# A graph network's edge pass: one gathered tile in 24 built from columns in SBUF, and gathers of 125 rows throughout

## The chip, the cores and the metric

The kernel runs on one core of a Trainium2 chip. The metric is the device time of one execution in microseconds; lower is better. A core has five engines with instruction streams of their own: PE (TensorE, matmul), DVE (VectorE), ACT (ScalarE), POOL (GpSimd) and SP (SyncE). Here SP issues the plain transfers and POOL the indirect ones; 16 DMA engines carry both.

## The reference

12,500 nodes with 64 features, 412,500 edges with 32 features, sorted by receiver. With h the normalised and rectified node features:

```python
def _L0_gnn_ref(node_features, edge_features, senders, receivers, W1, b1, W2, b2, Wa1, ba1, Wa2, ba2, Wu1, bu1, Wu2, bu2):
    act = jax.nn.swish
    msg_in = jnp.concatenate([node_features[senders], node_features[receivers], edge_features], axis=-1)
    messages = act(msg_in @ W1 + b1) @ W2 + b2
    att_logits = act(msg_in @ Wa1 + ba1) @ Wa2 + ba2
    att = jax.nn.softmax(att_logits, axis=0)
    messages = messages * att
    aggregated = jax.ops.segment_sum(messages, receivers, num_segments=node_features.shape[0])
    upd_in = jnp.concatenate([node_features, aggregated], axis=-1)
    return act(upd_in @ Wu1 + bu1) @ Wu2 + bu2
h = jnp.maximum(_layernorm(x, axis=-1), 0.0)
x = x + _L0_gnn_ref(h, edge_attr_32, src, dst, ...)
```

The softmax runs over all edges, so the kernel keeps a running maximum. All data are float32.

## The kernel before

**Tables.** A node phase computes h and keeps its transpose in SBUF (`hT`, the even and the odd nodes on either half of the partitions). It writes two tables of 128 columns to DRAM: `ts_d`, what a node gives as a sender, and `tr_d`, what it gives as a receiver. The 128 columns are 64 of the attention's first layer and 64 of the message's.

**Groups.** The edges are cut into tiles of 125 (`EP`); 8 tiles (`K`) make a group, and there are 413 groups (`NG`). `one_pass` runs over them.

**`load(g)`** (L524) is called two groups ahead. It takes one of 7 `gather` buffers, and POOL issues 8 indirect transfers into it (L533), one for each tile j: row e of tile j is the row of `ts_d` that edge e's sender names. Even j fetch 125 rows, odd j 126 (`WIDE`); the row in excess falls on a partition that nothing reads. POOL runs ahead of all other engines until there is no free buffer; a buffer is free when `end` of its group has read it. In every fourth group SP loads edge features into `eo` (L544) and receivers into `dbs` (L547). For each group SP loads two windows of `tr_d` into `wins` (L554), one of three buffers, at an address that a register holds. DVE compares the receivers with the window's rows (L558), which gives a one-hot matrix in `eo`; on PE four products (L562, each in two instructions) of `eo` with `wins` give, in the PSUM tile `pe`, the receivers' and the edges' part for all 8 tiles.

**`begin(g)`** (L570): DVE adds `pe` to the gathered rows (L573), ACT takes the tanh into `pe` (L576). **`end(g)`** (L578): DVE makes the messages (L586) and the attention logits (L592, L594, L597); in every fourth group `top` and `weigh` move the running maximum, with two exponentials on ACT (L627, L630).

**`sum_up`** (L714) sums an earlier group by node: `by_node` builds weights on DVE (L640) and multiplies them on PE into `sp` (L646); `out_of` copies `sp` with ACT (L652); `project` multiplies by W2 and Wu1 on PE (L657); `put` adds on DVE to `sums` (L671, L675) and notes the maximum in `stand` (L678), both at register addresses.

**Order.** Most instructions are kept in the order in which they are written (`pin`); each engine works through its own in that order. In an iteration of the loop (L738) ACT has the tanh, the copy of `out_of`, the first `burst`, the second `burst`, and `weigh`'s exponentials where a batch ends.

**Columns.** `chosen` names groups whose last tile (j = 7) is not gathered. `numbers(g)`, `places(g)`, `columns`, `burst` and the branches on `g in chosen` in `load` and `begin` serve them. In this kernel `chosen` is empty (L472), and none of this issues an instruction.

Of the kernel before, what the change touches and what calls it, by code (L numbers as in the profile page):

```python
# [44 lines left out]
F32 = mybir.dt.float32  # L45
# [8 lines left out]
P = 128  # L54
EP = 125
# [3 lines left out]
C = 2 * U  # L59
S1 = U + 1  # L60
K = 8
# [12 lines left out]
EVERY = 3  # L74
PHASE = 1
SLOTS = (((0, 24), (24, 24)), ((48, 24), (72, 12)), ((84, 24), (108, 17)))
ROUND = 12582912.0
WIDE = 126
EPS = 1e-5
NEG = -3.0e38  # L80
BIG = 3.0e38
# [9 lines left out]
def gnn_kernel(ctx: ExitStack, tc: tile.TileContext, n_edges, x, src, src_row, dst, dst_row, first, edge,  # L91
# [73 lines left out]
    with tc.tile_pool(name="node1", bufs=1) as node1, \  # L165
# [134 lines left out]
        for c, nn in chunks:  # L300
            tr = node.tile([P, CB, C], F32, name="tr")[:, :nn, :]
            for b in range(0, nn, 4):
                n = min(4, nn - b)
                pn = node_ps.tile([P, 4, C], F32, name="pn", bufs=4)
                for i in range(0, n, 2):
# [7 lines left out]
        pin(nc.scalar.dma_start(hT_d, hT))  # L313

    one_pass(tc, n_edges, locals())
    again = nc.values_load(wrong[0:1, 0:1], min_val=0, max_val=1,
                           skip_runtime_bounds_check_because="it is the outcome of a comparison")
# [76 lines left out]
def one_pass(tc, n_edges, v):  # L394
    nc = tc.nc
    NB, T, NG, NP, NT = (v[k] for k in ("NB", "T", "NG", "NP", "NT"))
    ident, iota_w, bj, dloc, src_full, base_sb, real, unreal, far, wrong = (
        v[k] for k in ("ident", "iota_w", "bj", "dloc", "src_full", "base_sb", "real", "unreal",
                       "far", "wrong"))
    ts_d, tr_d, bq_d, xb_d, edge, dst_row = (  # L400
        v[k] for k in ("ts_d", "tr_d", "bq_d", "xb_d", "edge", "dst_row"))
    wa2, ba2_c, w2b, wu1a, wu2h, we, gather = (
        v[k] for k in ("wa2", "ba2_c", "w2b", "wu1a", "wu2h", "we", "gather"))
# [8 lines left out]
    with ExitStack() as ctx:  # L412
# [38 lines left out]
        for w in wins:  # L451
            nc.vector.memset(w, 0.0)
            for r in range(2):
                rows = slice(WR + r * DE, WR + (r + 1) * DE)
                nc.vector.tensor_copy(w[rows, :, r, :], we[rows, None, :].to_broadcast([DE, 2, C]))
        with tc.tile_pool(name="work2", bufs=2) as work2, \
# [3 lines left out]
            pes, gss, lgs, ps_, psums, sps, pps, ees, mts, nums, cols = ({} for _ in range(11))  # L460
# [8 lines left out]
            for h in range(2):  # L469
                nc.vector.tensor_copy(w2u[:, h, :], w2u_ps)  # L470

            chosen = set()  # L472

            def numbers(g):
                if g in chosen:
# [30 lines left out]
            def burst(g, k):  # L506
                for i in range(EVERY):
# [6 lines left out]
                           ap=[[C, NP + WR - SHIFT], [SHIFT * C, 2], [1, C]])  # L514

            def registers(g, engine, at, base=base_sb, top=NP - 1):
                n = min(NQ, NG + (base is not base_sb) - g)
                _, regs = nc.values_load_multi_w_load_instructions(
                    base[0:1, g:g + n], engines=[engine], min_val=0, max_val=top,
                    skip_runtime_bounds_check_because=WHY)  # L520
                for i in range(n):
                    at[g + i] = regs[i]

            def load(g):  # L524

                t = g * K
                if g % NQ == 0:
                    registers(g, ENG.SP, at_sp)
                full = gather.tile([P, K, C], F32, name="gs")
                gs = gss[g] = full[:EP]  # L530
                for j in range(K - (g in chosen)):
                    rows = WIDE if j % 2 == 1 else EP
                    nc.gpsimd.indirect_dma_start(  # L533
                        out=full[:rows, j, :], out_offset=None, in_=ts_d[:, :],
                        in_offset=bass.IndirectOffsetOnAxis(ap=src_full[:rows, t + j:t + j + 1], axis=0))
                if g % NQ == 0:
                    n = min(NQ, NG - g) * E2
                    eo = eos[g // NQ % 2]
                    i = g // NQ % 2
                    db = dbs[i * WR:(i + 1) * WR].bitcast(I32)  # L540
                    for i in range(g, min(g + NQ, NG)):
                        e = slice((i - g) * E2, (i - g + 1) * E2)
                        ees[i] = eo[:, e], db[:, e]
                    nc.sync.dma_start(eo[WR:, :n],  # L544
                                      edge[:, g * E2:g * E2 + n])
                    for r in range(2):
                        nc.sync.dma_start(  # L547
                            db[r * R:(r + 1) * R, :n],
                            bass.AP(tensor=dst_row.tensor, offset=dst_row[r:r + 1, g * E2:].offset,
                                    ap=[[0, R], [1, n]]))  # L550
                eo, db = ees.pop(g)
                win = wins[g % WINS]
                for r in range(2):
                    nc.sync.dma_start(win[r * R:(r + 1) * R, :, r, :],  # L554
                                      tr_w[bass.ds(at_sp[g], R), :, :])
                for h in range(2):
                    e = slice(h * E2 // 2, (h + 1) * E2 // 2)
                    pin(nc.vector.tensor_scalar(eo[:WR, e], db[:, e], bj[g // NQ % 2 * WR:(g // NQ % 2 + 1) * WR, g, h:h + 1], None,  # L558
                                                op0=ALU.is_equal))
                pe = pes[g] = pre_ps.tile([P, K, C], F32, name="pe")[:EP]  # L560
                for q in range(H):
                    pin(nc.tensor.matmul(pe[:, 2 * q:2 * q + 2, :], eo[:, q * EP:(q + 1) * EP],  # L562
                                         win[:, q // 2, :, :], start=True,
                                         stop=q < H - 1 or g not in chosen))
                if g in chosen:
                    to, _ = cols[g]
                    pin(nc.vector.scalar_tensor_tensor(to, nums[g], half, to, op0=ALU.is_equal, op1=ALU.mult))
                    pin(nc.tensor.matmul(pe[:, K - 1, :], to, stack, start=False, stop=True))
# [166 lines left out]
            for g in range(AHEAD):  # L735
                load(g)
            done = 0
            for g in range(NG):  # L738
# [18 lines left out]
                if g + AHEAD < NG:  # L757
                    load(g + AHEAD)
# [382 lines left out]
```

## Time and profile before

| | us |
|---|---|
| median of 3 runs | 5168.84 |
| the 3 runs | 5172.98, 5157.05, 5168.84 |
| the profiled execution | 5172.98 |
| its span, first to last instruction | 5171.3 |

| engine | busy us | share of the span | instructions |
|---|---|---|---|
| POOL | 3674.5 | 71% | 3329 |
| DVE | 3165.5 | 61% | 8745 |
| PE (matmul) | 2470.4 | 48% | 11247 |
| PEld (weight loads, beside matmul) | 1946.3 | 38% | 11247 |
| ACT | 608.2 | 12% | 1250 |

The mean granted TensorE clock is 0.595; the DMA engines are some 30% busy. "Busy" leaves out register, semaphore and DMA-issuing instructions of the sequencers, but counts POOL's indirect transfers, for which POOL itself works. In the page's lines of groups, the two numbers after the bar are the busy time in us and the mean of one instruction in ns; after the second bar stands the idle time of the engine just before them, and what ended it. In a timeline the columns are start and length in us, engine, line, operation, tiles, count, and in brackets the idle time before it.

### The profile page before, as it was taken

The numbers are of one execution on the slowest core, as the hardware profiler recorded it, in microseconds if no ns is written. First come the engines' busy times: TensorE is split into PE (matmuls) and PEld (weight loads), VectorE is DVE, ScalarE is ACT, GpSimd is POOL, SyncE is SP. The second block draws the span as 40 slices with busy tenths as digits, with TensorE's granted clock in tenths as the row PEclk, the third lists the DMA queues.
The fourth block names the chain that finished last, engine by engine and source line by source line (L and its number), as shares of the span: only waits on it lengthen the run. The fifth ranks groups of instructions, "written<-read, shape, count | busy, mean of one in ns | idle before, by whom it ended". The sixth has DMA issues, their size and how long they took to land. (4 is left out here: it accounts for less than half of the span.)

```text
span 5171.3 us, 46541 instructions
## 1 busy us (share of the span) xinstructions
PE 2470.4 (48%) x11247; PEld 1946.3 (38%) x11247; DVE 3165.5 (61%) x8745; ACT 608.2 (12%) x1250; POOL 3674.5 (71%) x3329
## 2 busy tenths in 40 slices
PE   5254544544454544444544544444444444444545
PEld 4243433433343433333333433333333333333435
DVE  6366666666665656565655656665656555655757
ACT  3011111111110111111110111111111111110112
POOL 4777677677677677777777777777777777777772
PEclk8555565665555556665655556665656555655656
DMA  7233333333333323323323322322323323323322
GB/s 242 64 80 74 78 88 74 79 80 78 75 74 70 71 64 73 73 67 72 73 66 70 73 67 69 74 67 70 72 65 73 73 64 73 73 65 72 73 66 69
DMA packets 315703, 393.24 MB, mean 76 GB/s; under 512 B 153249, under 2 KB 244478, under 8 KB 315042
## 3 DMA queue, kind: packets, MB, share of 16 engines
q0 software_dynamic: 211456, 214.45, 17.8%
q1 hardware_dynamic: 102594, 166.10, 13.1%
q10 hardware_dynamic: 1376, 9.67, 0.5%
q8 instruction: 92, 1.51, 0.1%
q14 instruction: 185, 1.52, 0.1%
HBM read 362.26 MB, written 25.72 MB: 75 GB/s over the span
## 5 line engine op out<-in xcount | busy, mean ns | idle before, releaser
L533 POOL DMA_INDIRECT gs<-ts_d,src_sb x3304 | 3657.3, 1107 | 1410.1 <-issue 1377.3
L562 PE MATMUL pe<-wins,eo 128*125 128x256 f32 x3304 | 1497.2, 631 | 1055.7 <-issue 453.6
L562 PEld LDWEIGHTS pe<-wins,eo 128*125 128x125 f32 x3304 | 1000.4, 317 | 1348.9 <-issue 518.5
L657 PE MATMUL mt<-ss,w2u 65*128 65x40 f32 x826 | 224.4, 369 | 1336.6 <-issue 703.3
L657 PEld LDWEIGHTS mt<-ss,w2u 65*128 65x128 f32 x826 | 209.4, 293 | 1536.3 <-issue 970.7
L640 DVE TENSOR_SCALAR wt<-iota_w,dloc,p 125x40 f32<-125x40 f32 x3304 | 760.1, 342 | 5.0
L646 PE MATMUL sp<-wt,acts 125*65 125x40 f32 x6608 | 714.6, 286 | 3.6 <-DVE wt L640 2.7
L646 PEld LDWEIGHTS sp<-wt,acts 125*65 125x65 f32 x6608 | 678.9, 205 | 7.7 <-DVE wt L640 3.4
L675 DVE TENSOR_TENSOR sums<-sums,mt 64x40 f32 x606 | 116.0, 191 | 854.1 <-remote 734.0
L576 ACT ACTIVATE pe<-gs 125x1024 f32<-125x1024 f32 x413 | 424.7, 1028 | 1600.3 <-DVE gs L573 759.1
L573 DVE TENSOR_TENSOR gs<-pe,gs 125x1024 f32<-125x1024 f32 x413 | 503.1, 1218 | 50.3 <-issue 30.7
L671 DVE SCALAR_TENSOR_TENSOR sums<-sums,scale,mt 64x40 f32 x220 | 56.1, 255 | 594.5 <-remote 446.3
L652 ACT COPY ss<-sp 65x40 f32<-65x40 f32 x413 | 77.4, 187 | 2543.9 <-remote 2380.3
L592 DVE SCALAR_TENSOR_TENSOR pe<-pe,gs 125x512 f32<-125x512 f32 x413 | 288.9, 699 | 14.0
L594 DVE TENSOR_TENSOR pe<-pe,w_all 125x512 f32<-125x512 f32 x413 | 288.7, 699 | 13.8
L586 DVE SCALAR_TENSOR_TENSOR acts<-pe,gs 125x512 f32<-125x512 f32 x413 | 285.6, 692 | 15.7 <-issue 3.1
L597 DVE TENSOR_REDUCE lg<-pe 125x8 f32<-125x512 f32 x413 | 284.0, 688 | 11.0
L558 DVE TENSOR_SCALAR eo<-dbs,bj 64x250 f32<-64x250 int32 x826 | 274.4, 372 | 16.1 <-DMA dbs<-in_dst_row_dram 7.8
L678 DVE COPY stand<-nmax 64x40 f32 x826 | 181.8, 220 | 2.0 <-issue 1.4
L616 PE MATMUL mt<-ident,mx 125*128 125x125 f32 x110 | 46.4, 421 | 269.7 <-remote 124.5
L623 DVE TENSOR_REDUCE gm<-mt 128x1 f32<-128x125 f32 x110 | 31.1, 282 | 200.7 <-remote 200.1
L357 DVE TENSOR_SCALAR bu<-mt,w_all 64x256 f32<-64x256 f32 (+1 forms) x50 | 23.9, 478 | 170.0 <-remote 124.6
(113 smaller groups left out, 571.3 us busy)
## 6 DMA issues: line engine op xcount, KB each, us to landing
gs<-ts_d,src_sb POOLq DMA_INDIRECT x3304
eo<-in_edge_dram SPq DMA_DIRECT2D x103, 500.0 KB
dbs<-in_dst_row_dram SPq DMA_DIRECT2D x206, 250.0 KB
wins<-tr_d SPq DMA_DIRECT2D x826, 32.0 KB
ts_d<-ts SPq DMA_DIRECT2D x5, 896.0 KB
tr_d<-tr ACTq DMA_DIRECT2D x5, 896.0 KB
hT_d<-hT ACTq DMA_DIRECT2D x1, 3136.0 KB
xt<-in_x_dram SPq DMA_DIRECT2D x24, 128.0 KB
```

The costliest lines, as they stand in the source:

```text
L533: nc.gpsimd.indirect_dma_start(out=full[:rows, j, :], out_offset=None, in_=ts_d[:, :], in_offset=bass.IndirectOffsetOnAxis(ap=src_full[:ro ...
L558: pin(nc.vector.tensor_scalar(eo[:WR, e], db[:, e], bj[g // NQ % 2 * WR:(g // NQ % 2 + 1) * WR, g, h:h + 1], None, op0=ALU.is_equal))
L562: pin(nc.tensor.matmul(pe[:, 2 * q:2 * q + 2, :], eo[:, q * EP:(q + 1) * EP], win[:, q // 2, :, :], start=True, stop=q < H - 1 or g not in ...
L573: pin(nc.vector.tensor_tensor(gss[g][:, :n, :], pes[g][:, :n, :], gss[g][:, :n, :], ALU.add))
L576: pin(nc.scalar.activation(pes[g], gss[g], AF.Tanh))
L586: pin(nc.vector.scalar_tensor_tensor(acts[g % ACTS][:, :, 0:U], th[:, :, U:C], 1.0, gs[:, :, U:C], op0=ALU.add, op1=ALU.mult))
L592: pin(nc.vector.scalar_tensor_tensor(att, th[:, :, 0:U], 1.0, gs[:, :, 0:U], op0=ALU.add, op1=ALU.mult))
L594: pin(nc.vector.tensor_tensor(att, att, wa2[:EP, None, :].to_broadcast([EP, K, U]), ALU.mult))
L597: pin(nc.vector.tensor_reduce(lgs[s][:, k:k + K], att, AX.X, ALU.add))
L640: pin(nc.vector.tensor_scalar(wt[:, j, :], iota_w[:EP, j // H, :], dloc[:, g * K + j:g * K + j + 1], p[:, k + j:k + j + 1], op0=ALU.is_equ ...
L646: pin(nc.tensor.matmul(sp, acts[g % ACTS][:, j, :], wt[:, j, :], start=j == 0, stop=j == K - 1))
L657: pin(nc.tensor.matmul(pp, w2u.rearrange("s h u -> s (h u)"), sps.pop(g), start=True, stop=True))
```

## The change

Three things differ. `chosen` holds every third group from 10 to 400 (131 groups). All gathers have 125 rows, and a chosen group has 7 of them. With `chosen` filled, the code that stood idle issues instructions:

- `numbers(g)`, seven groups ahead: SP loads the tile's 125 sender numbers into all 128 partitions.
- `places(g)`, six groups ahead: six small DVE operations turn them into places in `hT` and keep each number's lowest bit.
- `columns`, in the `burst`s of the three iterations from five to three groups ahead: a register load for each burst, then for each of the 125 edges a copy by ACT of one column (128 partitions x 1) of `hT` into `cols`, at a register's address.
- in `load(g)`: DVE keeps the half of the column that is the sender's and zeroes the other (L567), and PE multiplies the 125 columns with the stacked sender weights, onto the same PSUM tile.
- in `begin(g)`: L573 adds 7 tiles, and the eighth is copied from PSUM.

```diff
-            chosen = set()
+            chosen = {g for g in range(8, NG - 12) if g % EVERY == PHASE}
```

```diff
-                full = gather.tile([P, K, C], F32, name="gs")
-                gs = gss[g] = full[:EP]
+                gs = gss[g] = gather.tile([P, K, C], F32, name="gs")[:EP]
                 for j in range(K - (g in chosen)):
-                    rows = WIDE if j % 2 == 1 else EP
                     nc.gpsimd.indirect_dma_start(
-                        out=full[:rows, j, :], out_offset=None, in_=ts_d[:, :],
-                        in_offset=bass.IndirectOffsetOnAxis(ap=src_full[:rows, t + j:t + j + 1], axis=0))
+                        out=gs[:, j, :], out_offset=None, in_=ts_d[:, :],
+                        in_offset=bass.IndirectOffsetOnAxis(ap=src_sb[:, t + j:t + j + 1], axis=0))
```

What both kernels hold, and only the second one runs (`EVERY` = 3, `PHASE` = 1; `SLOTS` deals out the 125 columns as 24 and 24, 24 and 12, 24 and 17):

```python
            def columns(g, first, n):
                if g not in chosen:
                    return
                to, at = cols[g]
                _, regs = nc.values_load_multi_w_load_instructions(
                    at[0:1, first:first + n], engines=[ENG.Activation], ...)
                for i in range(n):
                    pin(nc.scalar.copy(to[:, first + i:first + i + 1], hT[:, bass.ds(regs[i], 1)]))

            def burst(g, k):
                for i in range(EVERY):
                    columns(g + 3 + i, *SLOTS[EVERY - 1 - i][k])
...
                if g in chosen:
                    to, _ = cols[g]
                    pin(nc.vector.scalar_tensor_tensor(to, nums[g], half, to, op0=ALU.is_equal, op1=ALU.mult))
                    pin(nc.tensor.matmul(pe[:, K - 1, :], to, stack, start=False, stop=True))
...
                n = K - (g in chosen)
                pin(nc.vector.tensor_tensor(gss[g][:, :n, :], pes[g][:, :n, :], gss[g][:, :n, :], ALU.add))
                if n < K:
                    pin(nc.vector.tensor_copy(gss[g][:, n, :], pes[g][:, n, :]))
```

More of the change, by code (lines that the diff above doesn't have):

```diff
@@ L77 @@
 ROUND = 12582912.0
-WIDE = 126
 EPS = 1e-5
@@ L396, in one_pass @@
     NB, T, NG, NP, NT = (v[k] for k in ("NB", "T", "NG", "NP", "NT"))
-    ident, iota_w, bj, dloc, src_full, base_sb, real, unreal, far, wrong = (
-        v[k] for k in ("ident", "iota_w", "bj", "dloc", "src_full", "base_sb", "real", "unreal",
+    ident, iota_w, bj, dloc, src_sb, base_sb, real, unreal, far, wrong = (
+        v[k] for k in ("ident", "iota_w", "bj", "dloc", "src_sb", "base_sb", "real", "unreal",
                        "far", "wrong"))
```

## The prediction

> **What bounds the kernel now.** I read the page first: totals, then the costliest groups.
>
> ```profile
> span 5171.3 us, 46541 instructions
> ...
> DVE  6366666666665656565655656665656555655757
> ACT  3011111111110111111110111111111111110112
> POOL 4777677677677677777777777777777777777772
> ...
> L533 POOL DMA_INDIRECT gs<-ts_d,src_sb x3304 | 3657.3, 1107 | 1410.1 <-issue 1377.3
> ```
>
> No engine is full. POOL is closest to being occupied: 3304 gathers, 3657.3 us busy, and 1410.1 us idle which is put down to "issue", that is, to nothing the profile shows. ACT does about a tenth of what it could. So I read POOL's timeline, at the first gathers and at a later pause:
>
> ```profile
> 51.22 1.38 POOL L533 DMA_INDIRECT gs<-ts_d,src_sb  x1 [48.81 <-issue]
> 52.90 1.00 POOL L533 DMA_INDIRECT gs<-ts_d,src_sb  x1 [0.30 <-issue]
> 54.20 1.21 POOL L533 DMA_INDIRECT gs<-ts_d,src_sb  x1 [0.30 <-issue]
> 55.71 1.00 POOL L533 DMA_INDIRECT gs<-ts_d,src_sb  x1 [0.30 <-issue]
> ```
>
> ```profile
> 2543.36 1.21 POOL L533 DMA_INDIRECT gs<-ts_d,src_sb  x1 [0.30 <-issue]
> 2544.88 0.99 POOL L533 DMA_INDIRECT gs<-ts_d,src_sb  x1 [0.31 <-issue]
> 2552.61 1.21 POOL L533 DMA_INDIRECT gs<-ts_d,src_sb  x1 [6.73 <-issue]
> ```
>
> The first gather is j = 0 with 125 rows, and lengths alternate: 125 rows take 1.21 us, 126 rows 1.00 us, and 0.305 us always lies between two. So a 125-row gather costs 1.519 us of POOL (twice the mean of 1107 ns, less 1.00, plus 0.305) and a 126-row one 1.305. Of the idle time, 48.8 us stand before the first gather and 3303 x 0.305 = 1007 us are this spacing. The rest, 1410 - 49 - 1007 = 354 us, are pauses like the one of 6.73 us. They come at a group's first gather, the one that takes a buffer: POOL has filled all seven and waits for `end` of the group seven back.
>
> What keeps the buffers? On DVE, L573 opens every group's second half:
>
> ```profile
> 2507.77 1.22 DVE L573 TENSOR_TENSOR gs<-pe,gs 125x1024 f32<-125x1024 f32 x1 [0.21 <-issue]
> 2518.57 1.22 DVE L573 TENSOR_TENSOR gs<-pe,gs 125x1024 f32<-125x1024 f32 x1
> 2546.31 1.21 DVE L573 TENSOR_TENSOR gs<-pe,gs 125x1024 f32<-125x1024 f32 x1
> 2553.84 1.23 DVE L573 TENSOR_TENSOR gs<-pe,gs 125x1024 f32<-125x1024 f32 x1 [0.19 <-issue]
> 2561.68 1.23 DVE L573 TENSOR_TENSOR gs<-pe,gs 125x1024 f32<-125x1024 f32 x1 [0.21 <-issue]
> 2568.89 1.21 DVE L573 TENSOR_TENSOR gs<-pe,gs 125x1024 f32<-125x1024 f32 x1
> ```
>
> Steps of 10.8 and 27.7 us, then 7.5, 7.8, 7.2. The short steps are DVE's own work (3165 us over 413 groups is 7.7). The long steps are waits for TensorE:
>
> ```profile
> 2529.64 0.19 DVE L675 TENSOR_TENSOR sums<-sums,mt 64x40 f32 x1 [9.85 <-remote]
> 2621.73 0.19 ACT L652 COPY ss<-sp 65x40 f32<-65x40 f32 x1 [14.00 <-remote]
> 2644.58 0.19 ACT L652 COPY ss<-sp 65x40 f32<-65x40 f32 x1 [21.48 <-remote]
> ```
>
> Both read PSUM that PE has to finish. So two things share the pace. POOL needs 4 x (1.519 + 1.305) = 11.3 us a group. The chain behind runs at 7.2 to 7.9 in quick spells, catching POOL up, and in laggard spells falls back until POOL has no buffer. A pause ends where a quick spell begins (2546 to 2553), and so it repeats. The span is POOL's issue time plus the pauses:
>
> 51.2 (start of the first gather) + 3304 x 1.412 = 4665 + 354 + 102.5 (from the last gather's start at 5068.8 to the end) - 1.4 (the last one, counted twice) = 5171. That execution took 5172.98, 1.7 more than its span and 4.1 over the median of 5168.84.
>
> **The change part by part.**
> (a) Rows: all gathers have 125 rows, so each costs 1.519.
> (b) Fewer gathers: groups 10, 13, ... 400 are chosen, 131 of them, each one gather short: 3173. POOL then needs 3173 x 1.519 = 4820, which is 155 more than 4665: 1652 odd gathers get 0.214 longer (+354), and 131 go (-199). A group costs 11.67 instead of 11.3 on average. This lies on POOL's line with nothing beside it.
> (c) ACT gets 125 copies of one column (L503) in each chosen group, each with an instruction that sets the address, and 6 register loads. No such copy is in the trace. From below: L627 to L630 on ACT start 0.11 apart in the timeline (2507.59 and 2507.70). Nearer: four DVE operations with register addresses, L675 and L678, start at 2512.57, 2512.68, 2512.87 and 2512.99, 0.14 apart. From above: 187 ns of L652 with nothing overlapped and an address instruction of 0.07 before it, 0.26. I take 0.14, the row that has register addresses too. A load: 0.34 (L518 on DVE). So 125 x 0.14 + 6 x 0.34 = 19.5 us a chosen group (15.8 to 34.5), 6.5 for each group on average; ACT goes from 608 to 608 + 131 x 19.5 = 3160 us. In an iteration ACT has 1.03 (tanh) + 0.19 + 6.5 = 7.7, at most 8.7 where 48 copies fall. Behind the copies on ACT wait weigh's exponentials and the next tanh, for which DVE's `end` waits. With short steps of 7.5 this makes them 8 to 9, still under POOL's 11.67, and in long steps ACT idles 14 to 21 us already. Cost on the path: nothing, covered by POOL's pace; without that cover, some 1 us in each of about 5 short steps of 8, 260 us.
> (d) DVE gets in a chosen group 5 operations on 1x125 (0.2 from start to start, as L624 to L626), one on 128x125 and L567 on 128x125 (0.28 each, L623), and L573 split into 896 columns and a copy of 128 (0.22 for the copy, L678, less 0.13 by the slope between 692 ns at 512 and 1218 at 1024). 1.7 us, 131 times 223 us, from 3165 to 3388 us in all. It fills short steps: the same cover, and 223 us without it. L567 waits for the last columns of ACT; behind it on DVE are the weights L640 and then PE's sp matmuls. The columns stand ahead of the tanh that DVE needs anyway, so it is not late first.
> (e) PE gets one product more per chosen group, two instructions of 0.42 (L856, 128x128 f32): 110 us, under PE's idle half, but laggard spells are PE's: up to 110 us if none of it hides; from below nothing.
> (f) SP gets 131 loads of 62.5 KB (L478), 0.32 us of issue each as `wins` L554. They stand behind the windows and ahead of the next group's; the numbers are wanted one iteration later. Nothing, or 131 x 0.32 = 42 us.
>
> [...] The last gather is issued at 5068.8 and the last L573 starts at 5118.3, so landing has tens of us to spare.
>
> **The sum.** Span 51.2 + 4820 + 354 + 102.5 - 1.5 = 5326; as a run 5328, and 4 less against the median: **5325**, 3.0% slower. The pauses are kept as they are: I see no reason in the trace for PE's laggard spells to go.
>
> **The rivals.**
> *The pauses absorb it (the other side).* POOL waits 354 us for buffers. If the chain behind has a pace of its own, POOL's 155 us come out of these pauses: 5171, no change, as long as (c) to (e) hide. If 131 fewer gathers and a slower issue also calm PE, the pauses fall under 354 - 155 = 199 us, and it is faster: half the pauses gives 5150, none gives 4972; I take 5090. For it: the last L573 comes 48 us after the last gather's issue, so the chain never lacks data. Against: a chain that needs no gather would not follow POOL's pace so closely, and it gets work.
> *ACT becomes the bound.* At 0.26 a column an iteration needs 0.26 x 41.7 + 0.7 + 1.4 = 13 us, more than 11.67 + 0.9 of pauses; it decides from about 0.25. 413 x 13 and the 154 us at both ends give 5520, more where long steps stay on top. For it: ACT works in order, and its tanh stands behind up to 48 copies. Against: the 0.14 of the register rows.
> *DVE and PE on the path:* 223 and 110 onto 5325, 5400 to 5650; same side.
>
> **How the numbers follow.** Forecast 0.45 (5240 to 5420); work on the path, ACT or DVE, 0.22 (5420 to 5650); pauses absorb 0.33, of which 0.06 ends within 0.3% (16 us, about what a measurement of this kernel can tell from no change) and 0.27 under it. So faster 0.27, same 0.06, slower 0.67. Range 5090 to 5540: half of the faster cases lie under it (0.13), and the upper part of the ACT case (0.07) over it. The likeliest case alone: 5240 to 5420.
>
> **What would show it.** Gathers all at 1.21 with 0.305 between, 3173 of them; pauses near 354 us; L503 copies 0.14 apart and ACT busy 2.4 to 3.2 ms; short steps of L573 of 8 to 9 us with long steps of 18 to 28 left. Wrong, if the pauses are under 199 us, if columns are over 0.25 apart, or if long steps vanish or spread.

## The result, and the profile after

| | before | after |
|---|---|---|
| median, us (4 runs each) | 5167.32 | **4933.76** |
| lowest and highest | 5157.05, 5172.98 | 4932.87, 4935.06 |
| ratio after to before, 95% interval | | **0.955** (0.9534 to 0.9567) |

The change made the kernel 4.5% faster; the forecast was 3% slower, and the time lies under its range. The profiled execution after took 4935.06 us. From the gathers on, after's line numbers are lower by 3 (L530 is the gather, L570 the addition of L573, L672 and L668 the additions of L675 and L671). The page after:

```profile
span 4933.3 us, 81829 instructions
...
L530 POOL DMA_INDIRECT gs<-ts_d,src_sb x3173 | 3853.9, 1215 | 1020.6 <-issue 962.4
...
L503 ACT COPY cols<-hT 128x1 f32 x16375 | 1630.2, 189 | 754.3 <-issue 749.8
...
L570 DVE TENSOR_TENSOR gs<-pe,gs 125x1024 f32<-125x1024 f32 (+1 forms) x413 | 487.5, 1180 | 1153.1 <-DMA gs<-ts_d,src_sb 1140.2
...
L672 DVE TENSOR_TENSOR sums<-sums,mt 64x40 f32 x606 | 114.4, 189 | 4.7 <-issue 0.4
L668 DVE SCALAR_TENSOR_TENSOR sums<-sums,scale,mt 64x40 f32 x220 | 55.8, 254 | 78.4 <-PE mt L654 59.6
```

POOL's idle time fell from 1410.1 to 1020.6 us: some 50 before the first gather, 3172 spacings of 0.305 (967), and 3 us of pauses where there were 354. The last two lines tell where the pauses came from. These are the same two on the page before, which the forecast did not read:

```profile
L675 DVE TENSOR_TENSOR sums<-sums,mt 64x40 f32 x606 | 116.0, 191 | 854.1 <-remote 734.0
...
L671 DVE SCALAR_TENSOR_TENSOR sums<-sums,scale,mt 64x40 f32 x220 | 56.1, 255 | 594.5 <-remote 446.3
```

In front of them DVE idled 854.1 + 594.5 = **1449 us** before, and 4.7 + 78.4 = **83 us** after. Both additions wait for `mt`, PE's product of the sums. DVE's waits give the counterpart (us in total, times, longest). Before:

```profile
DVE sums L675 <- remote: 734.0, 120, 17.9
...
DVE gs L573 <- DMA gs<-ts_d,src_sb: 14.6, 47, 5.1
```

and after:

```profile
DVE gs L570 <- DMA gs<-ts_d,src_sb: 1140.2, 303, 7.9
```

Before, DVE hardly ever waited for gathered rows; after, that is nearly all it waits for. So the kernel after is bound by POOL's gathers, and the one before lost its 354 us of pauses to something that stood between PE and DVE. DVE's timeline after shows it as steps of the addition that opens a group's second half:

```profile
2498.07 1.09 DVE L570 TENSOR_TENSOR gs<-pe,gs 125x896 f32<-125x896 f32 x1 [3.55 <-DMA gs<-ts_d,src_sb]
...
2510.20 1.23 DVE L570 TENSOR_TENSOR gs<-pe,gs 125x1024 f32<-125x1024 f32 x1 [2.61 <-DMA gs<-ts_d,src_sb]
...
2526.09 1.23 DVE L570 TENSOR_TENSOR gs<-pe,gs 125x1024 f32<-125x1024 f32 x1 [7.87 <-DMA gs<-ts_d,src_sb]
...
2536.00 1.09 DVE L570 TENSOR_TENSOR gs<-pe,gs 125x896 f32<-125x896 f32 x1
```

Steps of 12.1, 15.9 and 9.9 us, the wait being for rows. Over all groups, 112 steps were longer than 15 us before, up to 32 and once 49; after, 35 are, the longest 16.

### The profile page after: what moved, and what is told of

Its sections match the earlier page's. It is cut to its first block, busy times and chain, and to the rows that moved or that the text cites. A ratio compares the mean times of both kernels' runs of the same rounds, so it can differ in the third digit from the quotient of the medians.

```text
span 4933.3 us, 81829 instructions
## 1 busy us (share of the span) xinstructions
PE 2429.9 (49%) x11509; PEld 1950.7 (40%) x11509; DVE 3456.5 (70%) x9793; ACT 2214.0 (45%) x17625; POOL 3871.1 (78%) x3198
## 5 line engine op out<-in xcount | busy, mean ns | idle before, releaser
L530 POOL DMA_INDIRECT gs<-ts_d,src_sb x3173 | 3853.9, 1215 | 1020.6 <-issue 962.4
L559 PE MATMUL pe<-wins,eo 128*125 128x256 f32 x3304 | 1524.4, 637 | 1551.2 <-DVE eo L555 1288.7
L503 ACT COPY cols<-hT 128x1 f32 x16375 | 1630.2, 189 | 754.3 <-issue 749.8
L570 DVE TENSOR_TENSOR gs<-pe,gs 125x1024 f32<-125x1024 f32 (+1 forms) x413 | 487.5, 1180 | 1153.1 <-DMA gs<-ts_d,src_sb 1140.2
L573 ACT ACTIVATE pe<-gs 125x1024 f32<-125x1024 f32 x413 | 424.8, 1029 | 1768.2 <-DVE gs L570 859.2
L643 PE MATMUL sp<-wt,acts 125*65 125x40 f32 x6608 | 652.2, 270 | 13.2 <-DVE wt L637 9.2
L643 PEld LDWEIGHTS sp<-wt,acts 125*65 125x65 f32 x6608 | 612.5, 185 | 23.6 <-DVE wt L637 14.0
L654 PE MATMUL mt<-ss,w2u 65*128 65x40 f32 x826 | 188.3, 322 | 262.8 <-DVE gm L620 199.4
L555 DVE TENSOR_SCALAR eo<-dbs,bj 64x250 f32<-64x250 int32 x826 | 303.2, 397 | 17.9 <-DMA dbs<-in_dst_row_dram 8.5
L613 PEld LDWEIGHTS mt<-ident,mx 125*128 125x128 f32 x110 | 20.0, 182 | 655.8 <-issue 652.2
L675 DVE COPY stand<-nmax 64x40 f32 x826 | 217.1, 263 | 3.3
L672 DVE TENSOR_TENSOR sums<-sums,mt 64x40 f32 x606 | 114.4, 189 | 4.7 <-issue 0.4
L668 DVE SCALAR_TENSOR_TENSOR sums<-sums,scale,mt 64x40 f32 x220 | 55.8, 254 | 78.4 <-PE mt L654 59.6
```

The lines of the kernel that those rows point to most:

```text
L503: pin(nc.scalar.copy(to[:, first + i:first + i + 1], hT[:, bass.ds(regs[i], 1)]))
L530: nc.gpsimd.indirect_dma_start(out=gs[:, j, :], out_offset=None, in_=ts_d[:, :], in_offset=bass.IndirectOffsetOnAxis(ap=src_sb[:, t + j:t ...
L570: pin(nc.vector.tensor_tensor(gss[g][:, :n, :], pes[g][:, :n, :], gss[g][:, :n, :], ALU.add))
L573: pin(nc.scalar.activation(pes[g], gss[g], AF.Tanh))
L643: pin(nc.tensor.matmul(sp, acts[g % ACTS][:, j, :], wt[:, j, :], start=j == 0, stop=j == K - 1))
L654: pin(nc.tensor.matmul(pp, w2u.rearrange("s h u -> s (h u)"), sps.pop(g), start=True, stop=True))
```

## The experiments

I call **held time** what DVE idles in front of the two additions, summed from their two lines. It parts the runs into two kinds, over 300 us and under 100, so the table comes first. A series is a set of kernels that ran beside one another on one chip; "beside" is the median of the kernel before in that series, and the ratio is to it.

| run | gathers, rows | beside | time | ratio (95%) | held time |
|---|---|---|---|---|---|
| *before* | 125 and 126 in turn | | 5167.3 | 1 | 1449 |
| *after* | 125 | 5167.3 | 4933.8 | 0.955 (0.953 to 0.957) | 83 |
| rows125 | 125 | 5327.5 | 5113.4 | 0.959 (0.956 to 0.963) | 44 |
| cols126 | 125 and 126 | 5327.5 | 5673.1 | 1.064 (1.060 to 1.068) | 629 |
| slow126 | 125 and 126 | 5327.5 | 5178.0 | 0.973 (0.969 to 0.978) | 1398 |
| seven125 | 125, 7 a group | 5327.5 | 4491.1 | 0.843 (0.839 to 0.846) | 44 |
| all126 | 126 | **4762.5** | 4411.8 | 0.926 (0.925 to 0.928) | 43 |
| odd127 | 125 and 127 | 4762.5 | 7340.6 | 1.541 (1.539 to 1.544) | 70 |
| odd128 | 125 and 128 | 4762.5 | 4698.8 | 0.987 (0.985 to 0.988) | 41 |
| fewer125 | 125 | 4762.5 | 4917.6 | 1.033 (1.031 to 1.034) | 44 |
| before2 | as before | 5317.2 | 5296.3 | 0.998 (0.995 to 1.001) | 1476 |
| after2 | 125 | 5317.2 | 4978.0 | 0.937 (0.932 to 0.942) | 328 |
| all126b | 126 | 5317.2 | 5711.9 | 1.074 (1.069 to 1.080) | 1867 |
| every2 | 125 | 5317.2 | 6487.2 | 1.221 (1.214 to 1.227) | 67 |
| rows125b | 125 | 5303.9 | 5113.2 | 0.963 (0.960 to 0.967) | 46 |
| tick126 | 126 | 5303.9 | 6046.1 | 1.139 (1.135 to 1.143) | 1759 |
| all128 | 128 | 5303.9 | 5734.4 | 1.080 (1.076 to 1.084) | 1582 |
| fewer125b | 125 | 5303.9 | 4917.6 | 0.927 (0.923 to 0.930) | 44 |
| pace126 | 126 | **4769.6** | 5607.9 | 1.176 (1.173 to 1.180) | 41 |
| rest126 | 126 | 4769.6 | 5014.0 | 1.052 (1.049 to 1.055) | 37 |

The kernel before itself has two times, with the same code: near 5300 in three series and 5167 in the first, and 4762 to 4770 in the two set in bold. This is no scatter within a series, and one chip showed both. I call the state of the four series with the longer time the bad condition.

### Rows alone, columns alone

**rows125**: the kernel before, all gathers of 125 rows, nothing else.

```diff
-                    rows = WIDE if j % 2 == 1 else EP
+                    rows = EP
```

> The kernel before with all gathers of 125 rows and no columns: part (a) alone. POOL issues 3304 x 1.519 = 5019 us, with the 152 us at both ends 5171. Theory ROWS (TensorE's long steps come from the transfers of 126 rows): long steps and pauses go, POOL sets the time alone, about 5130 to 5175. Theory PACE (the long steps go when POOL issues slowly enough for the chain to lack data): the same, 5130 to 5175. Theory COLUMNS (they go because ACT's column copies or the eighth tile's own path change the chain): long steps and pauses stay at some 7% of POOL's time, 5400 to 5520.

It took 5113.4, some 17 us less than the two theories that fit had expected. Its page:

```profile
L533 POOL DMA_INDIRECT gs<-ts_d,src_sb x3304 | 3996.6, 1210 | 1058.6 <-issue 961.8
...
L675 DVE TENSOR_TENSOR sums<-sums,mt 64x40 f32 x606 | 114.2, 188 | 4.7 <-issue 0.6
```

POOL is busy 339 us longer than in the kernel before, and yet rows125 is 4.1% faster: the 854.1 us in front of L675 are 4.7. No column is needed for that.

**cols126**: the columns in every third group, odd gathers still of 126 rows.

```diff
-            chosen = set()
+            chosen = {g for g in range(8, NG - 12) if g % EVERY == PHASE}
```

> The kernel before with the columns in every third group: odd gathers of 126 rows stay. POOL issues 1652 x 1.519 + 1521 x 1.305 = 4494 us, with both ends 4646. ROWS: long steps of L573 (over 15 us) and POOL pauses of over 200 us stay, 4850 to 5050. PACE: POOL is even quicker than in the kernel before, so the chain falls behind it as before: 5000 to 5250. COLUMNS: no long steps, POOL alone, 4600 to 4700.

It took 5673.1, 6.4% slower and over all three expectations. Its page:

```profile
L533 POOL DMA_INDIRECT gs<-ts_d,src_sb x3173 | 3520.2, 1109 | 2049.9 <-issue 1970.1
...
L675 DVE TENSOR_TENSOR sums<-sums,mt 64x40 f32 x606 | 115.4, 190 | 549.5 <-remote 477.0
```

Of POOL's idle time 1034 us are pauses. So columns on top of 126-row gathers cost much, and the 125 rows are what turns the change into a gain. They are not the whole gain. rows125 took 5113 us in both series in which it ran, the kernel after 4934 and 4978; the step between is the 131 gathers that POOL need not issue, 131 x 1.519 = 199 us, less what the columns cost. Beside a kernel before at 5300 the rows alone bring some 200 us. In the first series, with the kernel before at 5167, they would have brought 54 of the 234 us (an estimate, since rows125 did not run there).

### Pace

**slow126**: a memset of 128 x 128 on POOL, into the buffer, ahead of each group's gathers. **seven125**: seven gathers of 125 rows in every group, 10.6 us of POOL a group; it leaves out the sender's part of the eighth tile.

```diff
+                nc.gpsimd.memset(full[:, 0, :], 0.0)
```

```diff
-                for j in range(K - (g in chosen)):
-                    rows = WIDE if j % 2 == 1 else EP
+                for j in range(K - 1):
+                    rows = EP
...
-                n = K - (g in chosen)
+                n = K - 1
```

> The kernel before with a POOL memset of 128x128 into the buffer ahead of each group's gathers, which adds some 0.3 to 0.5 us of POOL time to a group; 126 rows stay, no columns. POOL then needs 11.6 to 11.8 us a group, as in the changed kernel. PACE: pauses and long steps go, 413 x 11.7 + 152 = 4980. ROWS: they stay, 5200 to 5350. COLUMNS: they stay, 5200 to 5350.

> All groups gather 7 tiles of 125 rows, no columns; the sender's part of each group's eighth tile is left out. POOL needs 413 x 7 x 1.519 = 4391 us (10.6 a group), with both ends 4543: quicker than in the kernel before. ROWS: no long steps over 15 us, 4500 to 4600. PACE: the chain falls behind, long steps and pauses come back, 4900 to 5200. COLUMNS: as PACE.

slow126 keeps its held time (1398 us) and 111 steps of over 15 us. At 5178.0 it lies 22 us under what ROWS had expected and far over PACE's 4980:

```profile
L676 DVE TENSOR_TENSOR sums<-sums,mt 64x40 f32 x606 | 116.0, 191 | 835.1 <-remote 757.8
```

seven125 asks more of the chain behind than the kernel before does, and has 44 us held and one step over 15 us (15.5). A slower POOL is not what frees DVE, at least not as the mean rate of a group.

### Other row counts, and a series without held time

**all126**, **odd127** and **odd128** set the rows of all or of the odd gathers (odd127 has 127 where odd128 has 128); **fewer125** is the kernel after without the columns' work, with the same 131 groups of seven gathers, whose eighth tile has no sender's part.

```diff
-                    rows = WIDE if j % 2 == 1 else EP
+                    rows = WIDE
```

```diff
-WIDE = 126
+WIDE = 128
```

```diff
-            chosen = {g for g in range(8, NG - 12) if g % EVERY == PHASE}
+            chosen = set()
+            fewer = {g for g in range(8, NG - 12) if g % EVERY == PHASE}
...
-                for j in range(K - (g in chosen)):
+                for j in range(K - (g in fewer)):
```

> The kernel before with all gathers of 126 rows, no columns. POOL issues 3304 x 1.305 = 4312 us, with both ends 4464. ROWS (126-row transfers bring TensorE's long steps): twice as many of them, so steps over 15 us at least as frequent as in the kernel before (some 110 of 413) and the time at 5170 or above. If only the alternation of 125 and 126 mattered: no long steps, 4500 to 4650.

> The kernel before with odd gathers of 127 rows in place of 126. [...] ROWS in the form that any other row count than 125 disturbs: long steps as before, 5170 to 5350.

> [...]

> The changed kernel without the columns' work: the same 131 groups gather 7 tiles of 125 rows, but numbers, places, copies and the extra product are left out, and with them the sender's part of these tiles. If the columns' work is hidden under POOL: the changed kernel's time, 4915 to 4940. If the copies delay the chain: faster by what they cost, down to 4880. If the columns help the chain: slower, 4980 or more.

Here the kernel before took 4762.5 and none of the four kernels had more than 70 us held, whatever its rows: my theory that 126 rows are bad by themselves had fallen. all126 and odd127 missed all that was expected of them, odd128 took 4698.8, 1.3% under the kernel before beside it, and fewer125 came as expected of hidden columns' work. Without held time every kernel here is POOL's issue time and two ends. The kernel before: 51 + 4665 + some 50 (an estimate, since no profile of it was kept here). fewer125 is then slower than before, by 155 us or 3.3%, which is the sign and the size that the forecast had worked out for POOL. all126 is the fastest full kernel of the study, 7.4% under the kernel before beside it.

### The same kernels once more

**before2**, **after2** and **all126b** are the three kernels unchanged. **every2** puts columns in every second group (bursts of 32, 31, 31 and 31).

```diff
-EVERY = 3
+EVERY = 2
...
-SLOTS = (((0, 24), (24, 24)), ((48, 24), (72, 12)), ((84, 24), (108, 17)))
+SLOTS = (((0, 32), (32, 31)), ((63, 31), (94, 31)))
```

> The kernel before once more, as it is, for a profile from this chip. Its time has been 5167 us on one chip, 5327 on a second and 4762 on a third. Theory CHIP+ROWS (on some chips 126-row transfers bring TensorE's long steps, on others nothing does): either 4755 to 4770 with no pauses of POOL and no step of L573 over 16 us, or 5150 to 5350 with 350 us of pauses or more. Theory DRIFT (a disturbance from outside that hits any kernel alike): the other three kernels move with it.

> The changed kernel once more. CHIP+ROWS: 4915 to 4940 whatever the chip, so 3.3% slower than the kernel before where that has no pauses, and 4 to 8% faster where it has. DRIFT: 3% slower or faster in step with the kernel before, its time between 4700 and 5100.

> All gathers of 126 rows once more. CHIP+ROWS: 4405 to 4420 on a chip where the kernel before has no pauses; on one where it has, long steps and pauses, 5100 or more.

> The changed kernel with columns in every second group (197 groups; bursts of 32, 31, 31, 31, four buffers for each of the three small tiles): 3107 gathers of 125 rows at 1.519 = 4719 us and 96 at both ends. If POOL alone sets the time: 4815 to 4840 on any chip. If ACT's copies (0.097 each as the changed kernel's profile shows, 12.1 us a chosen group) delay the chain now: 4850 to 4950.

The kernel before was at 5317 again, and all126, byte for byte the same, went from 4411.8 to 5711.9. Its pages, first all126 and then all126b:

```profile
L533 POOL DMA_INDIRECT gs<-ts_d,src_sb x3304 | 3292.0, 996 | 1055.3 <-issue 954.1
...
L675 DVE TENSOR_TENSOR sums<-sums,mt 64x40 f32 x606 | 114.3, 189 | 4.5 <-PE mt L657 0.4
```

```profile
L533 POOL DMA_INDIRECT gs<-ts_d,src_sb x3304 | 3297.4, 998 | 2323.0 <-issue 2260.9
...
L675 DVE TENSOR_TENSOR sums<-sums,mt 64x40 f32 x606 | 115.6, 191 | 1369.9 <-remote 1284.9
```

POOL's gathers and DVE's additions take as long in all126b as in all126; of the 1319 us between the two spans, 1268 are pauses that follow the held time. all126b's timeline shows one hold:

```profile
2035.29 0.65 PE L657 MATMUL mt<-ss,w2u 65*128 65x40 f32 x2 [5.59 <-issue]
...
2035.73 1.96 PE L646 MATMUL sp<-wt,acts 125*65 125x40 f32 x16
2036.50 0.99 POOL L533 DMA_INDIRECT gs<-ts_d,src_sb  x1 [0.30 <-issue]
...
2044.31 1.00 POOL L533 DMA_INDIRECT gs<-ts_d,src_sb  x1 [0.30 <-issue]
2045.61 1.00 POOL L533 DMA_INDIRECT gs<-ts_d,src_sb  x1 [0.30 <-issue]
2047.70 1.35 SPq L554 DMA_DIRECT2D wins<-tr_d  x2
2049.83 0.19 DVE L675 TENSOR_TENSOR sums<-sums,mt 64x40 f32 x1 [17.12 <-remote]
...
2050.22 0.19 ACT L652 COPY ss<-sp 65x40 f32<-65x40 f32 x1 [13.81 <-remote]
```

PE's records of the product for L675 end at 2035.94, those of the sums for L652 at 2037.69. DVE and ACT, which wait for nothing else, start at 2049.83 and 2050.22. In between POOL issues eight gathers, and the results come through 1 to 4 us after the last one, when POOL has no buffer left. The trace's semaphore events say that it is the signals that are late, and not PE's work: no raise of PE's semaphore is recorded between 2034.97 and 2047.69, and then nine from 2049.81 on, 0.04 us apart, while the two products of L646 behind each signal take PE 0.22 there. Of the 121 waits of over 4 us in front of the two additions, 103 ended in a pause of POOL.

In all126b that makes a circle: signals of PE hardly come through while POOL gathers, their lack keeps DVE from freeing buffers, and the lack of buffers stops POOL. There it is mostly the pauses that let the kernel go on. The kernel before is not in this circle: of its 143 waits of over 4 us only 18 ended in a pause, and in slow126 none of 144. There the signals are late too, but come through in the midst of the gathers. Of 208 additions that started over 1.5 us after the end of their product, 100 did so in the stretch behind a 125-row gather's start, 94 behind a 126-row one's and 14 in pauses; so it was not the 125-row gathers in particular that let them through.

The two traces of all126 differ in one more way. A trace also records raises of semaphores, of PE and the other engines and of landed transfers. Of the raises by landed transfers, all126's holds 71,922 and all126b's 18,393, for the same program and the same 262,852 packets; of PE's 3619 they hold 3531 and 3043. The six kept traces of the series with the fast kernel before have 71,000 to 73,500 landings and at least 3529 raises of PE. The fourteen of the other series have 17,000 to 54,400 and at most 3441, also where nothing was held (rows125 54,343; fewer125b 51,995, against fewer125's 71,251). So the bad condition can be told from the trace alone, and it was there in the runs that went well with 125 rows. It also means that a raise which is not recorded may have happened; the starts of DVE and ACT above do not depend on that.

**after2** (4978.0, over the 4940 that was expected; 328 us held) shows how 125-row gathers get by. Of PE's 3015 recorded raises that fell between the starts of two gathers 1.52 us apart, 96% came 0.5 to 0.9 us after the first start or later than 1.2, in 47% of the time. In fewer125, where nothing was held anywhere, the same stretches had 49%. So in this condition PE's signals keep time with POOL's gathers, and in after2 each gather has two places at which they get through. In the other 125-row kernels of the bad condition this is weaker: 65 to 67% in rows125, rows125b, fewer125b and seven125, 78% in the kernel after.

**every2** has little held time, and a slowness of its own (at most 4950 had been expected):

```profile
L503 ACT COPY cols<-hT 128x1 f32 x24500 | 2402.4, 187 | 3251.7 <-issue 3246.5
```

ACT is the bound: 2402 us of copies and 3246 us of "issue" in front of them. That idle time is the register load at the head of each burst (min, median and longest in ns):

```profile
L499 ACTq TENSOR_LOAD <-to x784: 1712/4326/7045, 121.6 to 6293.1; - x196
```

By their place the four loads of a group have medians of 1.98, 2.39, 6.72 and 6.76 us. The two dear ones begin at words 63 and 94, the others at 0 and 32. In the kernel after, where bursts begin at words 0, 24, 48, 72, 84 and 108, 24 words take 1.49, 17 words 1.28 and 12 words 0.78. With 17.8 us of loads and 125 x 0.097 = 12.1 of copies (24 take 2.33) in two groups, ACT has little room in the 31.4 us that two groups took.

### Rows or distance

**rows125b** and **fewer125b** repeat two kernels, **all128** has 128 rows in every gather, and **tick126** is all126 with a memset of one element after each gather.

```diff
+                    tick = small.tile([1, 1], F32, name="tick", bufs=1)
+                    nc.gpsimd.memset(tick, 0.0)
```

> The kernel before with all gathers of 125 rows, a second time. Theory ROWS (126-row gathers issued back to back hold PE's results back, 125-row gathers let them through): VectorE's idle time before L671 and L675 stays under 100 us, no long POOL pauses, 5090 to 5130 us whatever the kernel before takes beside it. Rival CHANCE (some executions are disturbed, whatever the rows): over 500 us of that idle time if the kernel before has it beside it.

> all126 with a memset of one element on POOL after each gather. Where the kernel before is at about 5300 us: theory PACE (PE's results need POOL to leave its gathers alone for some tenths of a us now and then): VectorE's idle time before L671 and L675 falls from the 1867 us of all126b to under 300, and the time to 4700 to 5100 us. Theory ROWS: over 1000 us of that idle time remains, 5400 us or more. Where the kernel before is at about 4760 us both give 3304 times the new period, 4600 to 5000 us.

> The kernel before with every gather of 128 rows (the period of the 128-row gathers of odd128 was 0.95 + 0.30 us; 3304 of them are 4140 us, about 4250 with the ends, unless VectorE's 3165 us and its waits set more). Where the kernel before is at about 5300 us: theory ROWS in the form that 126 rows alone are bad: no held results, 4250 to 4500 us. Theory PACE (the faster POOL issues, the longer results are held): worse than all126b, 5700 us or more.

> The kernel after without the columns' work, its 131 groups left with seven gathers (the sender part of the eighth tile is left out there). POOL's issue is the same as in the kernel after: 4900 to 4935 us if the columns' work is hidden, whatever the kernel before takes. If the columns' work is what brought the change its time, over 5050.

The kernel before took 5303.9. The two 125-row kernels take the same time as in their other series to 0.2 us (5113.4 and 5113.2; 4917.55 and 4917.58), with nothing held, and the other two are caught in holds. So it is not chance: over all series the seven runs in the bad condition whose gathers all have 125 rows have 44 to 328 us held, the seven others 629 to 1867. all128's page:

```profile
L675 DVE TENSOR_TENSOR sums<-sums,mt 64x40 f32 x606 | 115.5, 191 | 1362.7 <-PE mt L657 577.3
```

128 rows issue faster still (0.95 us) and are no better than 126. That is against the theory that 126 rows alone are bad, and as PACE had expected (5700 or more), so the rows and the distance between gathers are still not told apart: all gathers with little held time in the bad condition are also the ones 1.52 us apart. tick126 tells less than meant: its memsets (0.095 us each) were scheduled ahead in long rows, the gathers stayed 1.305 apart, and it is one more all126 with 312 us of memsets on top.

**pace126** and **rest126** were to put the 126-row gathers at the distance of the 125-row ones, and the same rest in one piece per group.

```diff
+                    tick = small.tile([P, 240], F32, name="tick", bufs=1)
+                    nc.gpsimd.memset(tick, 0.0)
```

```diff
+                tick = small.tile([P, 1700], F32, name="tick", bufs=1)
+                nc.gpsimd.memset(tick, 0.0)
```

> All gathers of 126 rows, each followed by a POOL memset of 128 x 240, which should put about 1.5 us between the starts of two gathers, as the 125-row gathers have. Where the kernel before is at about 5300 us: theory DISTANCE (PE's results get through where gathers are 1.52 us apart): under 150 us of VectorE's idle time before L671 and L675, no long POOL pauses, about 3304 x 1.52 + 110, 5050 to 5200 us. Theory ROWS (the 125-row gather itself lets them through): over 1000 us of that idle time, 5500 us or more. Where the kernel before is at about 4760 us both give 5050 to 5200.

> All gathers of 126 rows, with one POOL memset of 128 x 1700 ahead of each group's eight, about 1.7 us of rest per group (413 x 1.7 = 702 us), so the same mean rate as rows125. Where the kernel before is at about 5300 us: theory MEAN RATE (the held results are let through in any rest that is long enough, once per group): under 300 us of that idle time and 5050 to 5200 us. Theories DISTANCE and ROWS: over 700 us of it and 5400 us or more.

Neither could answer: the kernel before was at 4769.6, nothing was held, and pace126's memsets (0.30 us each) again stood in a row in front of eight gathers (its 5607.9 is over the 5200 expected). Whether a 126-row gather would let the signals through if it came every 1.52 us was therefore not tried.

## Why the prediction was wrong, step by step

- **POOL's gathers (a, b): right.** 3173 of them, 1.21 us each with 0.305 between. From the first start at 51.9 to the last at 4875.7 are 4823.8 us; the forecast had 4820.
- **"The pauses are kept as they are: I see no reason in the trace for PE's laggard spells to go."** This step failed. The pauses went from 354 to 3 us, and the end after the last gather from 102.5 to 57.6, as the chain no longer lags when POOL is done. By parts: 4818.5 + 354 = 5172.5 of gathers and pauses became 4823.8 (349 less), and the end lost 45; the 0.7 later start added, 5326 - 393 = 4933, the measured span. All else in the sum was within a few us.
- **Why it failed.** The long steps were read as PE working late. The records speak against it: in all126b PE had long done its products when DVE and ACT went on. In the kernel before, an addition of L671 or L675 that found DVE idle started 3.4 us (median) after the end of its product, up to 8.9; in rows125 0.7, at most 1.6. What was late was the signal. The runs tie that to POOL's gathers, the very instruction that the change touches, though not how. The page before had the trace of this in 1449 us of idle time on two lines, 1180 of them put down to "remote"; I quoted one such wait and named PE.
- **"The pauses absorb it": right side, wrong measure.** It asked for pauses under 199 us, and thought of "half" or "none". With none it gave 4972, 0.8% over the time; the rest is the end.
- **ACT (c): right total by two errors.** The columns start 0.093 us apart (median), not 0.14, and the loads of 24 words take 1.49 us, not 0.34:

```profile
2501.16 2.33 ACT L503 COPY cols<-hT 128x1 f32 x24 [0.61 <-issue]
2504.68 1.68 ACT L503 COPY cols<-hT 128x1 f32 x17 [1.20 <-issue]
```

  ACT's busy time rose by 2214 - 608 = 1606 us, and 750 us of "issue" stand in front of the copies: 18.0 us a chosen group against 19.5. The 0.11 between L627 and L630, the forecast's lower row, was nearer. The bracket of 0.61 and 1.20 is what a load leaves uncovered.
- **DVE, PE and SP (d, e, f): hidden, as said.** DVE rose by 291 us (223 forecast; 77 of it are L678, L558 and L640, which took longer each). fewer125 without the columns' work takes 4917.6 against 4933.8, so all of it costs some 16 us (the two ran in different series; fewer125b gave the same time).
- **"Long steps of 18 to 28 left": wrong,** none is.
- **Landings, beside the issue rows: they differ with the rows as well.** By packets of data, a gather of 125 rows moves 15 of 4096 bytes and 5 of 512 (rows125), one of 126 rows 14 of each (all126); one of 127 rows moves 16 of 2 to 8 KB (odd127). In the kernel before, the last data packet ended 2.9 us (median) after the start of a 125-row gather's issue and 2.3 after a 126-row one's (packets of data taken in the order of the gathers). POOL's pace hid that.

**What stays open.** That signals of PE come late while POOL issues gathers, and little so when all of them have 125 rows, was seen in every series where it could show. Whether the rows or the 1.52 us between the gathers do it was not told apart. What connects the two engines was not found, nor what turns the condition on: the same kernel on the same chip took 4412 and 5712. The missing raises show that recording goes differently in the bad condition (18,393 landings in all126b against 71,922 in all126). Every run on record was recorded, with its span and clock, so that the recording itself holds the signals is a rival that stays untested.

In the other condition the change costs time: after's 4934 against the 4762 of the kernel before there would be 3.6% (an estimate, since the two were never run beside one another; fewer125 was, and lost 3.3%). No version wins in both. all126 has the best time, 4412, and goes to 5712; the kernel after lies between 4934 and 4978, where the condition is the bad one, and is the best full kernel there.

## What to carry to other kernels

When an engine idles for a "remote" signal, compare its start with the end of the instruction that it waits for: here 3.4 us between them (the median in the kernel before) meant that the signal was late and not the work, and the cure lay on an engine that was neither of the two. An instruction that costs its own engine more can make the faster kernel: here 0.21 us more on every second gather brought 4% beside a kernel before at 5300. And a gain that rests on such an effect is only as good as the condition it was measured in; run the kernel before again, in another series, before believing a few per cent.

## What the runs showed of the hardware

- A gather's issue depends on its rows in no simple order: 1.21 us for 125, 1.00 for 126, 2.55 for 127, 0.95 for 128. By the packets of the gathers' queue the order is plain: 80 for 125 rows, 48 for 126, 272 for 127 and 32 for 128 (worked out from the queue's totals, rows125's 264320, all126's 158592, odd127's 581504 and odd128's 185024), so here the issue is the longer the more packets there are. 127 rows made the kernel 54% slower.

```profile
q0 software_dynamic: 581504, 227.76, 17.3%
...
L533 POOL DMA_INDIRECT gs<-ts_d,src_sb x3304 | 6222.9, 1883 | 1056.8 <-issue 1012.6
```

  These are odd127's; its mean of 1883 ns is that of 1.21 and 2.55.
- ACT's register loads cost 0.06 to 0.08 us a word in the bursts of the kernel after and in every2's at words 0 and 32, and 0.22 in every2's at words 63 and 94.
- SP had more long instructions where signals were held: 331 of them took 0.60 to 0.76 us in the kernel before (1449 us held), 44 in the kernel after (83 us).
